# Second layer's tails in small pieces with ScalarE a block behind VectorE, and the third layer's scaled nodes made in those tails

## The chip, the cores and the metric

One core of one Trainium2 chip runs the whole kernel. The metric is the device time of one execution in microseconds (us). Every time of a whole kernel below is the median of several executions in the fast state (no run of this study was slow); every profile is one fast execution. The engines are named as the profile names them: PE is TensorE's matmuls, PEld its weight loads, DVE is VectorE, ACT is ScalarE, POOL is GpSimd, SP is SyncE, which in these kernels only issues transfers. `SPq` and `ACTq` are the instruction queues in which SyncE and ScalarE issue DMA.

## The reference

Four graph layers over 4096 nodes of 128 features and a dense 4096 x 4096 adjacency of zeros and ones, each followed by a residual and a layer norm. The change touches the second layer (attention with four heads) and the start of the third (a normalised graph convolution).

```python
def _L1(x, adj, Wq, bq, Wk, bk, Wv, bv, Ws, bs, Wb):          # second layer
    q, k, v = (x @ W + b, split into 4 heads of 32)
    attn = einsum('nhc,mhc->hnm', q, k) / sqrt(32)
    e = where(adj == 0, 0, exp(attn - rowmax))
    out = (e / e.sum(-1)) @ v
    x_r = x @ Ws + bs                                          # the skip term
    beta = sigmoid(concat([out, x_r, out - x_r]) @ Wb)
    return beta * x_r + (1 - beta) * out

def _L2(x, adj, weight):                                       # third layer
    deg = sum(adj + I, axis=1)
    d = (deg + 1e-8) ** -0.5
    return relu((d[:, None] * (adj + I) * d[None, :]) @ x @ weight)

x = layernorm(x + _L1(x, ...))
x = layernorm(x + _L2(x, ...))
```

## The kernel before

The second layer's attention runs over eight row blocks `I` of 512 nodes, each in 32 steps `jb` of 128 columns. The loop issues the scores two steps ahead of the sums (their lead), and hands one piece of the last row block's tail (a Python generator, one piece up to each `yield`) to every step. In the trace the engines take their instructions in the order in which this loop emits them: in the first tail ScalarE exponentiated scores that were there at 1144.18 us only from 1146.29, after a wait of 3.35 us at `be`, and TensorE began sums whose mask had ended at 1164.54 only at 1166.71, after scores that had waited 2.24 us for ScalarE. The last row block has no steps after it: its tail runs alone, and is called drained below. The passage from the last sums to the end of the third layer's first row is called the handover.

```python
def degree():                       # one half row block of adjacency, summed by ScalarE
    nc.scalar.activation(nat, nat, AF.Identity, accum_out=self.deg2[:, k, i : i + 1])
    row(n + 1)                      # the next load, into the same (single) buffer

def scores(I, jb):
    e = ep.tile([P, NH, S], F32, tag="e", name="e")
    for h2 in range(0, NH, 2):
        p = ps_s.tile([P, 2, S], F32, tag="s", name="ps")        # three buffers
        ...  # two matmuls
        nc.scalar.activation(e[:, h2 : h2 + 2, :], p, AF.Exp)
    nc.vector.scalar_tensor_tensor(e, at..., 0.0, e, op0=ALU.not_equal, op1=ALU.mult)   # the mask

def ending(I):                      # the tail of a row block
    ev = ...                        # ScalarE copies the sums out
    r = R[:, 4 * I : 4 * I + 4, :]  # the skip terms of this row block
    yield
    for a in range(2):
        ...  # 4 transposes, maximum, reciprocal, 4 products into o
        yield
    for b in range(4):
        ...  # two products with the gate's weights, summed into be
        yield
    nc.vector.tensor_tensor(be[:, 0, :], be[:, 0, :], be[:, 1, :], ALU.add)
    nc.scalar.activation(be[:, 0, :], be[:, 0, :], AF.Exp, scale=-1.0)       # waits for the line above
    yield
    ...  # the gate: 1 + be, reciprocal, 1 - be
    for b in range(4):
        ...  # X += r * beta + o * (1 - beta), then the row's mean and variance
        yield
    nc.vector.tensor_scalar(rs, self.mv[:, 4 * I : 4 * I + 4, 1], EPS_LN, None, op0=ALU.add)
    nc.scalar.activation(rs, rs, AF.Ln)                                      # waits for the line above
    nc.scalar.activation(rs, rs, AF.Exp, scale=-0.5)
    yield
    for b in range(4):
        ...  # X = (X - mean) * rs

for n in range(-LEAD, len(seq)):    # LEAD = 2
    I, jb = seq[n + LEAD]
    if jb % 4 == 3 and (I or jb > 8) or I == NS - 1 and jb in (13, 17):
        degree()
    scores(I, jb)
    I, jb = seq[n]
    sums(I, jb)
    next(rest, None)                # one piece of the tail
    if jb == NT - 1:
        rest = ending(I); next(rest)

def layer2(self, weight):           # the third layer
    nc.vector.tensor_scalar(d, d, 1.0, 1e-8, op0=ALU.add, op1=ALU.add)
    nc.scalar.activation(d, d, AF.Sqrt)
    nc.vector.reciprocal(d, d)
    for t in range(NT):             # 32 instructions
        nc.vector.tensor_scalar(Y[:, t, :], X[:, t, :], d[:, t : t + 1], None, op0=ALU.mult)
    for I in range(NS):
        ...  # 4 matmuls with the identity
        for J in range(NS):
            (nc.sync if J % 2 else nc.scalar).dma_start(out=at, in_=self.adjT[I, J])
            ...  # 4 matmuls pa += Y^T at
```

Of the kernel before, what the change touches and what calls it, by code (L numbers as in the profile page):

```python
# [16 lines left out]
P = 128  # L17
# [13 lines left out]
class Net:  # L31
# [737 lines left out]
    def layer1(self, Wq, bq, Wk, bk, Wv, bv, Ws, bs, Wb):  # L769
# [4 lines left out]
        with ExitStack() as ctx:  # L774
# [11 lines left out]
            R = keep.tile([P, NT, D], F32, tag="R", name="R")  # L786
# [81 lines left out]
    def attention_unshifted(self, VA, KS, QS, at0, stack, R, wb):  # L868
# [4 lines left out]
        with ExitStack() as ctx:  # L873
# [72 lines left out]
            def ending(I):  # L946
# [10 lines left out]
                for a in range(2):  # L957
# [6 lines left out]
                    nc.vector.reciprocal(sm[:, a, :, :], sm[:, a, :, :])  # L964
                    for b in range(4):
                        nc.vector.tensor_tensor(
                            o[:, b, :].rearrange("p (c h) -> p h c", h=NH)[:, 2 * a : 2 * a + 2, :],
                            pt[:, b, :].rearrange("p (g c) -> p g c", g=2)[:, :, 0:C],
                            sm[:, a, :, b].unsqueeze(2).to_broadcast([P, 2, C]),
                            ALU.mult,  # L970
                        )
                    yield
                for b in range(4):
                    for k, t in enumerate((o, r)):
                        junk = rot.tile([P, D], F32, tag="junk", name="junk")
                        nc.vector.scalar_tensor_tensor(
                            junk, t[:, b, :], 1.0, wb[k], op0=ALU.mult, op1=ALU.mult, accum_out=be[:, k, b : b + 1]
                        )
                    yield

                nc.vector.tensor_tensor(be[:, 0, :], be[:, 0, :], be[:, 1, :], ALU.add)
                nc.scalar.activation(be[:, 0, :], be[:, 0, :], AF.Exp, scale=-1.0)
# [3 lines left out]
                nc.vector.tensor_scalar(be[:, 1, :], be[:, 0, :], -1.0, 1.0, op0=ALU.mult, op1=ALU.add)  # L986
                for b in range(4):
                    x = X[:, 4 * I + b, :]
                    nc.vector.scalar_tensor_tensor(x, r[:, b, :], be[:, 0, b : b + 1], x, op0=ALU.mult, op1=ALU.add)
                    nc.vector.scalar_tensor_tensor(x, o[:, b, :], be[:, 1, b : b + 1], x, op0=ALU.mult, op1=ALU.add)  # L990
                    self.row_stats(4 * I + b)
                    yield
                nc.vector.tensor_scalar(rs, self.mv[:, 4 * I : 4 * I + 4, 1], EPS_LN, None, op0=ALU.add)
                nc.scalar.activation(rs, rs, AF.Ln)
                nc.scalar.activation(rs, rs, AF.Exp, scale=-0.5)
                yield
                for b in range(4):
# [3 lines left out]
                    )  # L1001

            seq = [(I, jb) for I in range(NS) for jb in range(NT)]
            LEAD = 2
            rest = iter(())
            with tc.manual_schedule():
# [33 lines left out]
            nc.vector.tensor_tensor(self.deg, self.deg2[:, 0, :], self.deg2[:, 1, :], ALU.add)  # L1040
# [106 lines left out]


    def layer2(self, weight):
        nc, tc, N, NT, NS, D, X = self.nc, self.tc, self.N, self.NT, self.NS, self.D, self.X  # L1150
        with ExitStack() as ctx:
            keep = ctx.enter_context(tc.tile_pool(name="keep2", bufs=1))
            rot = ctx.enter_context(tc.tile_pool(name="rot2", bufs=2))
            at2 = ctx.enter_context(tc.tile_pool(name="at2", bufs=8))
            ps_a = ctx.enter_context(tc.tile_pool(name="ps_a", bufs=2, space=PSUM))
            ps_b = ctx.enter_context(tc.tile_pool(name="ps_b", bufs=2, space=PSUM))
            Y = keep.tile([P, NT, D], F32, tag="Y", name="Y")
            w = self.load_mat(weight, "w2")

# [4 lines left out]
            for t in range(NT):  # L1164
                nc.vector.tensor_scalar(Y[:, t, :], X[:, t, :], d[:, t : t + 1], None, op0=ALU.mult)
            for I in range(NS):
# [11 lines left out]
                for J in range(NS):  # L1178
                    at = at2.tile([P, 4, S], F32, tag="at", name="at")
                    (nc.sync if J % 2 else nc.scalar).dma_start(out=at, in_=self.adjT[I, J])  # L1180
# [227 lines left out]
def tile_kernel(  # L1408
# [11 lines left out]
    net.layer1(Wq, bq, Wk, bk, Wv, bv, Ws, bs, Wb)  # L1420
    net.layer2(w2)
# [30 lines left out]
```

## Time and profile before

| what | value |
|---|---|
| time before the study | 2402.70 us, median of 3 runs (2401.38 to 2403.52) |
| profiled run | span 2398.1 us |
| busy share of the span | PE 84%, DVE 79%, ACT 61% |
| the second layer's attention | about 1022 to 1842 us of the span |
| a row block in it (copies `ev` to copies `ev`) | 102.5 to 102.9 us |
| last sums of the attention to the end of the third layer's first row | 57.9 us (1841.62 to 1899.51) |

The two rows of the page's costliest groups that matter most are TensorE's sums and scores in the second layer. The columns are line, engine, operation, tiles, shapes and count; then busy us and mean ns of one; then the idle time just before them with what ended it.

```profile
L937 PE MATMUL pv<-e,VA 128*64 128x512 f32 x2048 | 501.8, 611 | 8.0 <-DVE e L920 8.0
L911 PE MATMUL ps<-QS,KS 128*128 128x512 f32 x1024 | 315.1, 427 | 26.3 <-ACT e L918 24.2
```

Directly visible idle time of TensorE is only some 34 us. The change can be worth more than that: after 2.24 us of idle time in the first tail, eight sums took 2.84 us in place of 1.94, and that cost hides in the busy time. (Each of the code's four matmuls with sums is two records in the trace, hence eight; so it is with `pa`.) The lines that carry the argument from here are shown in the prediction; ScalarE's table load (`ACT_TABLE_LOAD`) at 1859.06, of which it speaks, took 1.28 us, and from 1130 to 1858 us, where the tails' Ln and Exp lie, there is none.

### The profile page before, as it was taken

The numbers are of one execution on the slowest core, as the hardware profiler recorded it, in microseconds if no ns is written. First come the engines' busy times: TensorE is split into PE (matmuls) and PEld (weight loads), VectorE is DVE, ScalarE is ACT, GpSimd is POOL, SyncE is SP. The second block draws the span as 40 slices with busy tenths as digits, with TensorE's granted clock in tenths as the row PEclk, the third lists the DMA queues.
The fourth block names the chain that finished last, engine by engine and source line by source line (L and its number), as shares of the span: only waits on it lengthen the run. The fifth ranks groups of instructions, "written<-read, shape, count | busy, mean of one in ns | idle before, by whom it ended". The sixth has DMA issues, their size and how long they took to land.

```text
span 2398.1 us, 24121 instructions
## 1 busy us (share of the span) xinstructions
PE 2018.2 (84%) x8795; PEld 1117.5 (47%) x8795; DVE 1901.2 (79%) x2695; ACT 1459.8 (61%) x1761; POOL 107.1 (4%) x146
## 2 busy tenths in 40 slices
PE   4477878778777761799999999999997899979998
PEld 4266666566666651533333333333332444444443
DVE  7478888788788888777787878778786877668887
ACT  5688899888888886478777787777875000010000
POOL 2000000000000042221000000000000000000000
PEclk7689989989898895799999999999999899989999
DMA  2455466564656530697464564645453877537884
GB/s 53 141 181 196 154 206 205 160 206 156 201 175 193 177 126 1 228 226 213 159 192 158 176 193 158 192 149 186 171 180 124 315 285 286 200 123 285 290 291 170
DMA packets 112869, 448.45 MB, mean 187 GB/s; under 512 B 9760, under 2 KB 20064, under 8 KB 71776
## 3 DMA queue, kind: packets, MB, share of 16 engines
q1 hardware_dynamic: 84944, 294.71, 36.3%
q10 hardware_dynamic: 18576, 135.27, 16.1%
q0 software_dynamic: 9216, 16.78, 3.9%
q8 instruction: 73, 1.20, 0.2%
q14 instruction: 60, 0.49, 0.1%
HBM read 369.10 MB, written 77.63 MB: 186 GB/s over the span
## 4 chain that ended last, share of the span: by engine, by line
PE 56%; DVE 25%; ACT 12%; issue 3%; DMA 2%; ACTq 0%; POOL 0%; SPq 0%; DVEq 0%; POOLq 0%
PE pv L937 15%; PE pa L1327 9%; PE pa L1182 9%; PE ps L911 9%; DVE e L920 5%; PE pz L583 4%; DVE w L606 3%; PE pi L674 3%; DVE w L636 3%; DVE t L632 3%; PE ptA L564 3%; ACT t L628 3%; ACT e L918 2%; ACT at L572 2%; ACT w L601 1%
## 5 line engine op out<-in xcount | busy, mean ns | idle before, releaser
L920 DVE SCALAR_TENSOR_TENSOR e<-at,e 128x2048 f32<-128x2048 f32 x256 | 581.6, 2287 | 169.0 <-ACT e L918 168.5
L918 ACT ACTIVATE e<-ps 128x1024 f32<-128x1024 f32 x512 | 489.2, 1025 | 132.0 <-PE ps L911 103.4
L937 PE MATMUL pv<-e,VA 128*64 128x512 f32 x2048 | 501.8, 611 | 8.0 <-DVE e L920 8.0
L911 PE MATMUL ps<-QS,KS 128*128 128x512 f32 x1024 | 315.1, 427 | 26.3 <-ACT e L918 24.2
L911 PEld LDWEIGHTS ps<-QS,KS 128*128 128x128 f32 x1024 | 172.2, 190 | 254.8 <-ACT e L918 167.1
L674 PE MATMUL pi<-HA,w 128*128 128x129 f32 x1152 | 188.1, 339 | 84.1 <-DVE w L636 84.1
L937 PEld LDWEIGHTS pv<-e,VA 128*64 128x64 f32 x2048 | 125.8, 137 | 252.6 <-issue 227.5
L1327 PE MATMUL pa<-w,F 128*128 128x512 f32 x512 | 223.8, 598 | 13.1 <-DVE w L1324 13.1
L1182 PE MATMUL pa<-at,Y 128*128 128x512 f32 x512 | 223.5, 597 | 4.1 <-DMA at<-adjT 4.1
L674 PEld LDWEIGHTS pi<-HA,w 128*128 128x128 f32 x1152 | 181.2, 251 | 94.4 <-DVE w L636 94.4
L1324 DVE SCALAR_TENSOR_TENSOR w<-rho,col,at 128x512 f32<-128x512 f32 x256 | 187.5, 747 | 19.3 <-PE pa L1327 2.3
L591 DVE SCALAR_TENSOR_TENSOR t<-ei,de,pz 128x512 f32<-128x512 f32 x144 | 107.4, 747 | 106.1 <-PE pz L583 102.3
L564 PE MATMUL ptA<-ident,ad 128*128 128x128 f32 x1032 | 145.8, 287 | 41.2 <-ACT at L572 34.1
L1192 DVE SCALAR_TENSOR_TENSOR odd<-at 128x2048 f32<-128x2048 f32 x64 | 146.5, 2290 | 37.8 <-DMA at<-adjT 37.2
L564 PEld LDWEIGHTS ptA<-ident,ad 128*128 128x128 f32 x1032 | 124.7, 148 | 97.5 <-ACT at L572 51.9
L572 ACT COPY at<-ptA 128x512 f32<-128x512 f32 x200 | 108.4, 588 | 98.7 <-PE ptA L564 98.5
L583 PE MATMUL pz<-HT 128*128 128x512 f32 x292 | 161.5, 664 | 4.9 <-DVE w L655 4.6
L1327 PEld LDWEIGHTS pa<-w,F 128*128 128x128 f32 x512 | 97.6, 192 | 135.0 <-issue 105.0
L1182 PEld LDWEIGHTS pa<-at,Y 128*128 128x128 f32 x512 | 97.6, 192 | 124.4 <-issue 119.5
L606 DVE TENSOR_TENSOR w<-w,at 128x2048 f32<-128x2048 f32 x64 | 143.7, 2281 | 0.0
L1331 ACT COPY a<-pa 128x512 f32<-128x512 f32 x8 | 4.7, 586 | 202.0 <-PE pa L1327 178.8
L903 ACT ACTIVATE nat<-nat 128x2048 f32<-128x2048 f32 x64 | 122.7, 1918 | 3.2 <-DMA nat<-in_adj_dram 3.2
(341 smaller groups left out, 2368.8 us busy)
## 6 DMA issues: line engine op xcount, KB each, us to landing
at<-adjT SPq DMA_DIRECT2D x127, 1024.0 KB, 4.8
at<-adjT ACTq DMA_DIRECT2D x65, 1024.0 KB, 4.9
ad<-in_adj_dram SPq DMA_DIRECT2D x64, 1024.0 KB, 6.4
adjT<-at SPq DMA_DIRECT2D x64, 1024.0 KB, 8.3
nat<-in_adj_dram ACTq DMA_DIRECT2D x64, 1024.0 KB, 4.9
qk<-cut SPq DMA_DIRECT2D x16, 512.0 KB, 11.7
KS<-qk POOLq DMA_DIRECT2D x32, 256.0 KB, 8.9
QS<-qk POOLq DMA_DIRECT2D x32, 256.0 KB, 8.5
```

The lines of the kernel that those rows point to most:

```text
L564: nc.tensor.transpose(pt[:, ib, :], st[p]["ad"][k][:, ib, jb * P : (jb + 1) * P], self.ident)
L572: copy(st[p]["at"][k][:, jb, :], st[p]["pt"].pop(m))
L583: nc.tensor.matmul(pz, lhsT=HT[:, j * P : (j + 1) * P], rhs=HT[:, I * S : (I + 1) * S], start=True, stop=True)
L606: nc.vector.tensor_tensor(w, w, at, ALU.mult)
L674: nc.tensor.matmul(self.po[ib // 2][:, ib % 2, :], lhsT=w[0][:, jb, ib * P : (ib + 1) * P], rhs=HA[:, 4 * J + jb, :], start=False, stop=(J ...
L911: nc.tensor.matmul(p[:, h, :], lhsT=KS[:, h2 + h, jb * P : (jb + 1) * P], rhs=QS[I % 2][:, h2 + h, :], start=True, stop=True,)
L918: nc.scalar.activation(e[:, h2 : h2 + 2, :], p, AF.Exp)
L920: nc.vector.scalar_tensor_tensor(e, at[:, jb % 4, :].unsqueeze(1).to_broadcast([P, NH, S]), 0.0, e, op0=ALU.not_equal, op1=ALU.mult,)
L937: nc.tensor.matmul(st["po"][h // 2][g : g + 64, :], lhsT=VA[:, o : o + 64], rhs=e[:, h, :], start=(jb == 0), stop=(jb == NT - 1), skip_gro ...
L1182: nc.tensor.matmul(pa, lhsT=Y[:, 4 * J + jb, :], rhs=at[:, jb, :], start=False, stop=(J == NS - 1 and jb == 3), skip_group_check=True,)
L1324: nc.vector.scalar_tensor_tensor(w, rho[:, I * S : (I + 1) * S], col[:, 0, j : j + 1], at[:, jb, :], op0=ALU.max, op1=ALU.mult)
L1327: nc.tensor.matmul(pa, lhsT=F[:, j, :], rhs=w, start=False, stop=(j == NT - 1), skip_group_check=True)
```

## The change

Its intent: no ScalarE instruction of a tail should have to wait for a VectorE instruction emitted in the same piece (ScalarE comes one step later, the lag of the runs below), no piece should be longer than what VectorE has free in a step, and the work in front of the third layer (degrees to the power -1/2, 32 scalings) should lie in the tails, where VectorE has room. The scaled nodes overwrite the skip terms `R`, which are dead by then, so they need no memory of their own. The description of the change counts 30 pieces; by the `yield`s there are 25, and 14 before, with the copies `ev` counted in both.

```diff
@@ the tail
                     nc.vector.reciprocal(sm[:, a, :, :], sm[:, a, :, :])
+                    yield
                     for b in range(4):
...
-                for b in range(4):
-                    for k, t in enumerate((o, r)):
+                for k, t in enumerate((o, r)):
+                    for b in range(4):
...
-                    yield
+                        if b % 2:
+                            yield
                 nc.vector.tensor_tensor(be[:, 0, :], be[:, 0, :], be[:, 1, :], ALU.add)
+                yield
                 nc.scalar.activation(be[:, 0, :], be[:, 0, :], AF.Exp, scale=-1.0)
                 yield
...  # yields also after the gate and between update and statistics of each row
-                nc.vector.tensor_scalar(rs, self.mv[:, 4 * I : 4 * I + 4, 1], EPS_LN, None, op0=ALU.add)
+                nc.vector.tensor_scalar(rs, self.mv[:, tl, 1], EPS_LN, None, op0=ALU.add)
+                nc.vector.tensor_tensor(d[:, tl], self.deg2[:, 0, tl], self.deg2[:, 1, tl], ALU.add)
+                nc.vector.tensor_scalar(d[:, tl], d[:, tl], 1.0, 1e-8, op0=ALU.add, op1=ALU.add)
+                yield
                 nc.scalar.activation(rs, rs, AF.Ln)
                 nc.scalar.activation(rs, rs, AF.Exp, scale=-0.5)
+                nc.scalar.activation(d[:, tl], d[:, tl], AF.Ln)
+                nc.scalar.activation(d[:, tl], d[:, tl], AF.Exp, scale=-0.5)
                 yield
...  # the normalisation in two pieces
+                for b in range(4):
+                    t = 4 * I + b
+                    if b % 2 == 0:
+                        yield
+                    nc.vector.tensor_scalar(R[:, t, :], X[:, t, :], d[:, t : t + 1], None, op0=ALU.mult)
@@ the third layer
-    def layer2(self, weight):
+    def layer2(self, weight, Y):                  # Y is R, now allocated outside the second layer
-            Y = keep.tile([P, NT, D], F32, tag="Y", name="Y")
-            nc.vector.tensor_scalar(d, d, 1.0, 1e-8, op0=ALU.add, op1=ALU.add)
-            nc.scalar.activation(d, d, AF.Sqrt)
-            nc.vector.reciprocal(d, d)
-            for t in range(NT):
-                nc.vector.tensor_scalar(Y[:, t, :], X[:, t, :], d[:, t : t + 1], None, op0=ALU.mult)
...
-                    (nc.sync if J % 2 else nc.scalar).dma_start(out=at, in_=self.adjT[I, J])
+                    (nc.scalar if J % 2 else nc.sync).dma_start(out=at, in_=self.adjT[I, J])
```

More of the change, by code (lines that the diff above doesn't have):

```diff
@@ L766, in pair_loop, with layer1 @@
                     step(p)
-    def layer1(self, Wq, bq, Wk, bk, Wv, bv, Ws, bs, Wb):
+    def layer1(self, Wq, bq, Wk, bk, Wv, bv, Ws, bs, Wb, R):
         nc, tc, N, NT, D, X = self.nc, self.tc, self.N, self.NT, self.D, self.X
@@ L785, in layer1 @@
             qk = self.dram.tile([2, 2, P, N], F32, tag="qk", name="qk")
-            R = keep.tile([P, NT, D], F32, tag="R", name="R")
             wb = [self.load_row(Wb[k * D : (k + 1) * D, 0], f"wb{k}") for k in range(3)]
@@ L972, in ending @@
                     yield
-                for b in range(4):
-                    for k, t in enumerate((o, r)):
+                tl = slice(4 * I, 4 * I + 4)
+                for k, t in enumerate((o, r)):
+                    for b in range(4):
                         junk = rot.tile([P, D], F32, tag="junk", name="junk")
@@ L990, in ending @@
                     nc.vector.scalar_tensor_tensor(x, o[:, b, :], be[:, 1, b : b + 1], x, op0=ALU.mult, op1=ALU.add)
+                    yield
                     self.row_stats(4 * I + b)
-                    yield
-                nc.vector.tensor_scalar(rs, self.mv[:, 4 * I : 4 * I + 4, 1], EPS_LN, None, op0=ALU.add)
+                    if b < 3:
+                        yield
+                nc.vector.tensor_scalar(rs, self.mv[:, tl, 1], EPS_LN, None, op0=ALU.add)
+                nc.vector.tensor_tensor(d[:, tl], self.deg2[:, 0, tl], self.deg2[:, 1, tl], ALU.add)
+                nc.vector.tensor_scalar(d[:, tl], d[:, tl], 1.0, 1e-8, op0=ALU.add, op1=ALU.add)
+                yield
                 nc.scalar.activation(rs, rs, AF.Ln)
                 nc.scalar.activation(rs, rs, AF.Exp, scale=-0.5)
+                nc.scalar.activation(d[:, tl], d[:, tl], AF.Ln)
+                nc.scalar.activation(d[:, tl], d[:, tl], AF.Exp, scale=-0.5)
                 yield
@@ L1001, in ending @@
                     )
+                    if b == 1:
+                        yield
+                for b in range(4):
+                    t = 4 * I + b
+                    if b % 2 == 0:
+                        yield
+                    nc.vector.tensor_scalar(R[:, t, :], X[:, t, :], d[:, t : t + 1], None, op0=ALU.mult)
             seq = [(I, jb) for I in range(NS) for jb in range(NT)]
@@ L1005, in attention_unshifted @@
             rest = iter(())
+            d = self.deg
             with tc.manual_schedule():
@@ L1039, in attention_unshifted @@
                     pass
-            nc.vector.tensor_tensor(self.deg, self.deg2[:, 0, :], self.deg2[:, 1, :], ALU.add)
     def attention_shifted(self, V, qk, R, wb, spare):
@@ L1146, in attention_shifted @@
             self.normalise()
-    def layer2(self, weight):
-        nc, tc, N, NT, NS, D, X = self.nc, self.tc, self.N, self.NT, self.NS, self.D, self.X
-        with ExitStack() as ctx:
-            keep = ctx.enter_context(tc.tile_pool(name="keep2", bufs=1))
-            rot = ctx.enter_context(tc.tile_pool(name="rot2", bufs=2))
-            at2 = ctx.enter_context(tc.tile_pool(name="at2", bufs=8))
-            ps_a = ctx.enter_context(tc.tile_pool(name="ps_a", bufs=2, space=PSUM))
-            ps_b = ctx.enter_context(tc.tile_pool(name="ps_b", bufs=2, space=PSUM))
-            Y = keep.tile([P, NT, D], F32, tag="Y", name="Y")
-            w = self.load_mat(weight, "w2")
             d = self.deg
@@ L1164, in layer2 @@
             for t in range(NT):
-                nc.vector.tensor_scalar(Y[:, t, :], X[:, t, :], d[:, t : t + 1], None, op0=ALU.mult)
+                nc.vector.tensor_scalar(R[:, t, :], X[:, t, :], d[:, t : t + 1], None, op0=ALU.mult)
+    def layer2(self, weight, Y):
+        nc, tc, N, NT, NS, D, X = self.nc, self.tc, self.N, self.NT, self.NS, self.D, self.X
+        with ExitStack() as ctx:
+            at2 = ctx.enter_context(tc.tile_pool(name="at2", bufs=8))
+            rot = ctx.enter_context(tc.tile_pool(name="rot2", bufs=2))
+            ps_a = ctx.enter_context(tc.tile_pool(name="ps_a", bufs=2, space=PSUM))
+            ps_b = ctx.enter_context(tc.tile_pool(name="ps_b", bufs=2, space=PSUM))
+            w = self.load_mat(weight, "w2")
+            d = self.deg
             for I in range(NS):
@@ L1419, in tile_kernel @@
     net.layer0(x, w0, b0, attw, attb)
-    net.layer1(Wq, bq, Wk, bk, Wv, bv, Ws, bs, Wb)
-    net.layer2(w2)
+    with tc.tile_pool(name="scaled", bufs=1) as pool:
+        Y = pool.tile([P, net.NT, net.D], F32, tag="Y", name="Y")
+        net.layer1(Wq, bq, Wk, bk, Wv, bv, Ws, bs, Wb, Y)
+        net.layer2(w2, Y)
     net.layer3(w3, b3, a_s, a_r, out)
```

## The prediction

> **What bounds the kernel now**
>
> I read the page's busy shares first. TensorE is busy 84% of the span and the chain that ended last is 56% TensorE, but these are averages over four layers. So I asked which stretch holds the changed lines. The second layer's attention runs from 1022 to about 1842 us in eight row blocks of 32 steps; each step makes scores (L911), exponentiates them on ScalarE (L918), masks them on VectorE (L920) and sums them (L937), with scores two steps ahead of sums. A finished row block's tail is carried by the steps of the next. The busy times by stretch (columns: stretch, then busy us and count on PE, weight loads, DVE, ACT, POOL; clock; DMA share; GB/s) show one row block's tail, then its quiet rest:
>
> ```profile
> 1174.00:1225.00 51.00, 51.00 (x206) 19.70 (x204) 39.16 (x18) 41.17 (x45) 2.14 (x4) 1.00 0.60 184
> 1225.00:1277.00 52.00, 48.18 (x190) 18.35 (x188) 42.98 (x69) 36.63 (x42) 0.00 (x0) 0.97 0.48 164
> ```
>
> In the quiet part TensorE has no gap: it is the bound, at 2.994 us a step (scores begin at 1173.23 and, 18 steps on, the pass ends at 1227.16 in the chain: 53.93 / 18). In the tail it idles 3.8 of 52 us and its clock dips to 0.97, though DVE (43) and ACT (37) have room. So the tail loses time by waits, not work. The timeline of the first tail shows which:
>
> ```profile
> 1145.99 0.15 DVE L981 TENSOR_TENSOR be<-be 128x4 f32<-128x4 f32 x1
> 1146.18 0.21 ACT L982 ACTIVATE be<-be 128x4 f32<-128x4 f32 x1 [3.35 <-DVE be L981]
> ...
> 1157.82 1.94 PE L937 MATMUL pv<-e,VA 128*64 128x512 f32 x8 [0.30 <-DVE e L920]
> ...
> 1164.45 0.16 DVE L993 TENSOR_SCALAR rs<-mv 128x4 f32<-128x4 f32 x1
> 1164.65 0.20 ACT L994 ACTIVATE rs<-rs 128x4 f32<-128x4 f32 x1 [5.62 <-DVE rs L993]
> ...
> 1166.05 0.72 PE L911 MATMUL ps<-QS,KS 128*128 128x512 f32 x2 [2.24 <-ACT e L918]
> 1166.71 2.84 PE L937 MATMUL pv<-e,VA 128*64 128x512 f32 x8
> ```
>
> The four-element ScalarE instruction stands behind a DVE instruction that itself stands behind a 2.29 us mask. ScalarE stands still for 3.35 and 5.62 us, no exponential is made, and TensorE starves 2.24 us, then runs slowly (2.84 us for eight matmuls that take 1.94). Lost against 2.994 us a step, from the starts of the scores: 0.92 at `be`, 1.24 over the X steps (3.37 to 3.45 us each: mask 2.2 plus four small instructions 1.17), 3.40 at `rs`, 0.69 in the slow step after: 6.25 us.
>
> The copies `ev` mark the same point of each row block: 1120.85, 1223.69, 1326.60, 1429.51, 1532.37, 1635.02, 1737.51, so periods of 102.84, 102.91, 102.91, 102.86, 102.65 and 102.49. Ideal is 32 x 2.994 = 95.81, plus 0.39 for each of two transpose groups that stay (1124.65 to 1128.03 is 3.38): 96.6. Excess: 6.2 on average, in all six. In the last row block, scores from 1737.90 to 1833.87 hold 8.4 us of excess: its degree sums come every second step, and each waits for its own single-buffered load.
>
> Last I read the handover to the third layer, in the chain in order of time and the timeline:
>
> ```profile
> 1853.04 0.04 ACT rs L995
> 1853.08 5.98 issue
> 1859.06 0.75 ACT L1162
> ...
> 1860.23 9.17 DMA at<-adjT
> 1869.40 0.04 issue
> 1869.45 30.92 PE pa L1182 x66
> ```
>
> ```profile
> SPq L1180 <- DVE X L989: 34.6, 1, 34.6
> ```
>
> The conditional ends, ScalarE needs 5.98 us to come to its next instruction, loads a table, issues adjacency block 0, and TensorE has that at 1869.45. SyncE, idle, waited 34.6 us for L989, the last reader of the skip terms R, before it issued blocks 1, 3, 5, 7 at 1851.76; these then shared the transfer rate with block 0, which took 9.17 instead of the usual 4.8 us.
>
> [...] DVE 83% and ACT 70% busy in the tail, bubbles on PE. [...] the trace has 1.28 us at 1859.06 and no load at the present Ln, so the new Ln and Exp cost no switch. [...] The trace has 5.98 us on ACT and 5.16 on DVE after the conditional; [...] the change leaves it.
>
> **The change part by part**
>
> *Smaller pieces.* I count 25 pieces by the yields (13 before, last two joined), so a tail still fits in 32 steps. The DVE budget of a step is 2.994 - 2.29 = 0.70 us. Pieces, by cadence in the trace: two X instructions 0.73 (1154.31 to 1155.06), statistics 0.45, two beta products 0.54, four `o` products 0.54, maximum and reciprocal 0.43, two normalisations 0.56, two scalings of the third layer 0.4 to 0.56. All but one fit, with the mask overlapping (2.17 + 0.73 = 2.9). The exception is last statistics, rs, and two degree instructions: 0.45 + 3 x 0.2 = 1.05, 0.35 over, while the next piece holds nothing for DVE. So the 1.24 goes.
>
> *ACT a block behind.* `be`: its sum is made a step earlier, and a degree sum (2.47 us) lies before the scores between, so ScalarE comes late enough: 0.92 goes. `rs`: now four instructions, 4 x 0.24 = 0.95. Here the step behind a degree sum is the bad one: worked from the quiet sequence at 1821 to 1837, exponentials run back to back after the degree sum, the two masks follow late, and rs with its two degree companions is ready about 1.3 us after ScalarE asks. ScalarE is about 1.4 late afterwards, of which the next degree step can hide some 0.6 to 0.8 (DVE's lead there over the sums, 1828.2 to 1829.01). I leave 0.8 of loss in each tail. Hence 6.2 - 0.8 = 5.4 in each of six row blocks: 32.
>
> *Last row block.* Its degree sums at steps 11, 13, 15, 17, 19 come 7.2 us apart (1766.57 to 1773.74) where two steps are 6.0: 4 x 1.2 = 4.7 stays lost, less about 1.5 of lead. 8.4 - 3.2 - 0.8 = 4.4. Together 36.8 us.
>
> *Scaling moved.* Y's 32 instructions (6.36 us at 1861.21), the Sqrt and its table load leave the path in front of layer three; 28 of the scalings and all but the last degree work lie in DVE slack. The last tail, drained with nothing beside it, gains 2 DVE degree instructions (0.4), 2 on ACT (0.48) and 4 scalings, so ScalarE ends about 0.9 later: 1854.2.
>
> *R in an outer pool, queues swapped.* SyncE no longer waits for R, only for what lies under the new buffers (V and the keys, last read by the sums that end at 1841.6), and has block 0. Estimate: blocks 0, 2, 4, 6 issued near 1843, 10 us at the 415 GB/s that the handover's slices reach, all there by 1854. TensorE does block 0 inside the tail. ScalarE issues block 1 at 1854.2 + 5.8 + 0.4 = 1860.4, alone on the rate: there at 1865.2. Seven blocks from there: 7 x 3.43 + 3.4 [...] = 1892.7, where the row ended at 1900.4: gain 7.7 on that clock; some doubt of the early issue, 7.
>
> Sum: 36.8 + 7 = 43.8, less some for what I did not see: 43. 2402.7 - 43 = 2359.7, so 2360.
>
> **The rivals**
>
> 1. *Waits move instead of going.* PSUM: the transposed sums now keep one of three score buffers over a yield, so two remain for about two steps more, next to the `ev` copies and a degree sum. For it: the weight loads of the scores already wait mostly for ACT (167 us over the run). Against: the same two-buffer steps in the present tail (1124 to 1137) run at 2.99. If it held and rs waited longer, 2 to 2.5 us a tail stay: total about 2369.
> 2. *Everything hides.* Loss per tail zero and the start as above: 37 + 5.5 + 8 = 50.5, so 2352. For it: DVE and ACT have 9 and 15 us of room in the tail; against: in-order ScalarE with degree sums every fourth step.
> 3. *The loads stay late.* If SyncE still waits until about 1852, block 1 shares the rate again: the handover brings 5 instead of 7, 2362. If TensorE also had to wait for the last scaled node, about 4.
> 4. *DVE becomes the bound of the tail*: 12 us of tail work plus 2 us new in 25 steps x 0.70 = 17.5 of room; an X step at 3.0 or 3.1 would cost 1 us a tail, 2366. Not slower than before.
>
> **Range and chances**
>
> The ceiling of about 51 us makes 2% (48 us, 2354.6) reachable only if nearly nothing is left; the likely residues give 33 to 47. Range 2351 to 2371. Faster by over 2%: 0.22; within: 0.76; slower: 0.02 (a false dependency by the shared tile, nothing in the code suggests one).
>
> **What would show it right or wrong**
>
> `ev` copies 97.0 to 98.0 us apart in the first six periods confirm the tails; 99 or more refutes. The `be` wait of ScalarE should be near 0, that of `rs` 1 to 1.5 in place of 5.62. X steps at 2.99. On the changed kernel's own clock the tails come out about 37 us earlier, so what counts at the handover is distance: SyncE's first adjacency load issued within 2 us of the last sums (10 us behind them now), TensorE on block 0 before ScalarE's first load, that load landing in about 4.8 us, and the first row of the third layer ending some 51 us after the last sums (1900.4 - 1841.6 = 58.8 now). I would be wrong in the large if third-layer matmuls of later rows, or the fourth layer, changed: I expect 29.36 us a row there, as now.

## The result, and the profile after

| | before | after |
|---|---|---|
| median | 2402.04 us (2399.61 to 2403.52, 4 runs) | 2357.77 us (2356.13 to 2360.83, 4 runs) |
| ratio | 1 | 0.9818 (95%: 0.9801 to 0.9835) |
| span of the profiled run | 2398.1 | 2354.3 |

A ratio here is the mean time of one kernel's fast runs over that of the other kernel's fast runs of the same rounds, so it is not quite the ratio of the medians quoted beside it. 1.8% faster falls within the 2% that the prediction called most likely, and 2357.8 is 2 us under the predicted 2360.

Two stretches of the changed kernel, one row block's tail and then its quiet part, with the columns of the two shown of the kernel before (those stand the other way round, the quiet part first, although the sentence above them names the tail first):

```profile
1122.00:1174.00 52.00, 52.00 (x213) 20.52 (x214) 44.39 (x59) 41.37 (x46) 0.00 (x0) 1.00 0.57 188
1174.00:1225.00 51.00, 50.88 (x208) 19.76 (x207) 42.25 (x37) 41.98 (x49) 2.14 (x4) 1.00 0.63 188
```

TensorE now has no gap in the tail either, 213 matmuls where a tail of before held 190, at full clock. The second stretch shows VectorE at 42.25 where before it had 39.16: the later pieces of the tail reach into it.

The timeline of one tail, the lines that answer to those of `be` and `rs` before:

```profile
1249.53 0.15 DVE L985 TENSOR_TENSOR be<-be 128x4 f32<-128x4 f32 x1
...
1250.89 0.20 ACT L987 ACTIVATE be<-be 128x4 f32<-128x4 f32 x1
...
1280.82 0.20 ACT L1005 ACTIVATE rs<-rs 128x4 f32<-128x4 f32 x1 [1.15 <-DVE rs L1001]
...
1281.08 1.94 PE L938 MATMUL pv<-e,VA 128*64 128x512 f32 x8
```

ScalarE comes to the gate 1.2 us after VectorE has made its sum, so the 3.35 us wait is gone; at `rs` 1.15 us of wait are left of 5.62, and the sums after it run at 1.94 us, not 2.84. The copies `ev` now stand 97.21 to 97.23 us apart.

The chain of waits at the handover, which showed `issue` 5.98, then 9.17 for the load, before:

```profile
1817.98 2.83 issue
...
1821.28 5.64 DMA at<-adjT
...
1827.06 25.79 PE pa L1200 x56
```

And in the timeline there, the first issue on SyncE's queue and what TensorE did (ScalarE's first load is the one at 1821.28 above):

```profile
1807.52 17.59 SPq L1198 DMA_DIRECT2D at<-adjT  x5
...
1813.36 5.15 PE L1200 MATMUL pa<-at,Y 128*128 128x512 f32 x8
...
1827.06 3.47 PE L1200 MATMUL pa<-at,Y 128*128 128x512 f32 x4 [8.55 <-DMA at<-adjT]
```

SyncE issues its first block 1.3 us after the last sums (1806.18), and TensorE multiplies block 0 inside the drained last tail. Then it stands still for 8.55 us, because the next block is on ScalarE's queue, and ScalarE is still in the tail and then in the 2.83 us after the conditional.

Where the 43.8 us between the two profiled runs lie, from the starts and ends of the same groups in both traces:

| stretch | before | after | difference |
|---|---|---|---|
| start to first copy `ev` | 1120.85 | 1121.46 | +0.61 |
| first to seventh `ev` (six row blocks) | 616.66 | 583.31 | -33.35 |
| seventh `ev` to the end of the last sums | 104.11 | 101.41 | -2.70 |
| last sums to end of the third layer's first row | 57.89 | 46.66 | -11.23 |
| the third layer's other rows | | | +0.86 |
| preparation of the fourth layer | 47.77 | 50.05 | +2.28 |
| fourth layer | | | -0.26 |
| sum | | | -43.79 |

The fourth layer's preparation runs the same matmuls in the same order, some of them slower: eight matmuls `psr` take 5.29 us in place of 3.68, seventeen transposes 3.54 in place of 2.33. In the runs below the eight take 3.68 or between 5.08 and 5.75, and both values occur among kernels with the change (3.68 where ScalarE's Ln comes later or where the lag is taken out, 5.31 where the degree sums are spread). The granted clock goes with it: 0.69 over the eight (2079.4 to 2084.8 us), where before it was 1.00 (2124.0 to 2127.7). What sets it apart is open.

### The profile page after: what moved, and what is told of

The parts are those of the page before. It is cut to its first block, busy times and chain, and to the rows that moved or that the text cites. A ratio compares the mean times of both kernels' runs of the same rounds, so it can differ in the third digit from the quotient of the medians.

```text
span 2354.3 us, 24080 instructions
## 1 busy us (share of the span) xinstructions
PE 2013.7 (86%) x8795; PEld 1118.5 (48%) x8795; DVE 1896.6 (81%) x2708; ACT 1463.7 (62%) x1777; POOL 106.9 (5%) x146
## 4 chain that ended last, share of the span: by engine, by line
PE 60%; DVE 21%; ACT 13%; issue 3%; DMA 2%; ACTq 0%; SPq 0%; POOL 0%; DVEq 0%; POOLq 0%
PE pv L938 16%; PE ps L912 10%; PE pa L1345 9%; PE pa L1200 9%; PE pz L583 4%; DVE w L606 3%; PE pi L674 3%; DVE t L632 3%; DVE w L636 3%; PE ptA L564 3%; ACT t L628 3%; ACT at L572 2%; ACT e L919 2%; DVE e L921 2%; ACT w L601 1%
## 5 line engine op out<-in xcount | busy, mean ns | idle before, releaser
L642 PE MATMUL ptz<-ident,t 128*128 128x128 f32 x448 | 68.7, 294 | 67.7 <-DVE w L655 45.8
## 6 DMA issues: line engine op xcount, KB each, us to landing
qk<-cut SPq DMA_DIRECT2D x16, 512.0 KB, 11.8
```

## The experiments

Twelve runs were made, in three groups, each group on one chip with the kernel before beside it. All results were correct.

### Group one: which half of the change does what, and which half of the tail's part

**Tails only.** The kernel before with the changed tail (small pieces and lag), without the degrees and the scalings in it, and with the third layer as before.

```diff
 # kernel before, ending(): the changed kernel's yields and order
-nc.vector.tensor_tensor(d[:, tl], self.deg2[:, 0, tl], self.deg2[:, 1, tl], ALU.add)   # and the other
-...                                                                                     # degree lines
-    nc.vector.tensor_scalar(R[:, t, :], X[:, t, :], d[:, t : t + 1], None, op0=ALU.mult)
```

> The kernel before with the small pieces and ScalarE one block behind, and nothing else of the change: the skip terms stay skip terms, the scaling and the queues of the third layer stay as they were. Theory (the gain is mostly waits of ScalarE and oversize pieces in the tails): the changed kernel's trace gives 33.4 us between the first and the seventh copy ev and 2.7 us in the last row block, so about 36, a little more because rs has two ScalarE instructions less behind it; ev about 97.1 us apart; ratio to before 0.985, and the handover takes as long as before (about 58 us from the last sums to the end of the first row of matmuls). Rival (the moved scaling is what carries the gain, the pieces only make room for it): under 15 us, ratio above 0.994.

Measured: 2363.51 us (2360.21 to 2373.26, 5 runs), ratio 0.9855 (0.9832 to 0.9879). The first six row blocks took 96.88 to 97.16 us each, the last 101.0 to the end of the last sums (before: 104.1), the handover 56.2 (before: 57.9). So the tails carry four fifths of the gain.

**Handover only.** The changed kernel with the coarse tails of before, without lag; the degrees join the `rs` piece, the scalings follow as one more piece.

```diff
 # changed kernel, ending(): the yields of before, then
+                yield
+                for b in range(4):
+                    nc.vector.tensor_scalar(R[:, t, :], X[:, t, :], d[:, t : t + 1], None, op0=ALU.mult)
```

> The changed kernel with the old coarse tail pieces and no extra block between VectorE and ScalarE, but with the scaled nodes made in the tails, R in the outer pool and the swapped queues. Theory: the handover gains the 11 us that the changed kernel's trace shows, and each of seven tails loses about 0.5 us more than before, because two more ScalarE instructions (0.45 us) stand in the rs wait: net about 7 to 8, ratio 0.9967, ev 103.3 to 103.5 us apart. Rival (the handover's gain is only the early start of block 0, or needs the new pieces): under 4 us net, ratio above 0.998.

Measured: 2395.15 us (2392.76 to 2402.62, 22 runs), ratio 0.9971 (0.9963 to 0.9979). Row blocks 102.83 to 103.23, a mean of 103.02 against 102.78 before, so the tails lost about half of what I had expected; handover 47.4 us. The two halves together, 1.45% + 0.29% = 1.74%, make 1.81% within their intervals: they hardly touch each other.

**Lag only.** The kernel before with nothing but two `yield`s.

```diff
                 nc.vector.tensor_tensor(be[:, 0, :], be[:, 0, :], be[:, 1, :], ALU.add)
+                yield
                 nc.scalar.activation(be[:, 0, :], be[:, 0, :], AF.Exp, scale=-1.0)
...
                 nc.vector.tensor_scalar(rs, self.mv[:, 4 * I : 4 * I + 4, 1], EPS_LN, None, op0=ALU.add)
+                yield
                 nc.scalar.activation(rs, rs, AF.Ln)
```

> The kernel before with two more yields only, one ahead of the Exp of be and one ahead of the Ln of rs, so that ScalarE comes one block behind VectorE; the pieces stay coarse. Theory (by my sum of the losses of a tail: be 0.92, rs 3.40 and 0.69, X steps 1.24): the be and rs losses go but for half a microsecond, the X steps stay at 3.37 us: 4.4 of 6.2 us a tail, with a smaller share in the last row block about 29 us in all, ratio 0.988, ev 98.5 us apart. Rival (VectorE's coarse pieces set the tail, the wait of ScalarE is only where it shows): under 12 us, ratio above 0.995.

Measured: 2364.26 us (2362.81 to 2367.38, 4 runs), ratio 0.9850 (0.9829 to 0.9870); row blocks of 97.04 us, every one of the first six. I had expected 98.5, because I believed the coarse pieces themselves to be too long for VectorE. They are (the masks of the update steps, in which X gets its rows, start 3.4 us apart), but TensorE loses almost nothing by it: two added lines do as much as the whole new tail.

ScalarE's two groups between 1122 and 1770 us show what is left of the waits, about 0.5 us a tail each:

```profile
L983 ACT ACTIVATE be<-be 128x4 f32<-128x4 f32 x7 | 1.4, 206 | 3.7 <-DVE be L981 3.7
...
L996 ACT ACTIVATE rs<-rs 128x4 f32<-128x4 f32 x7 | 1.4, 206 | 3.6 <-DVE rs L994 3.6
```

**No lag.** The changed kernel without those two `yield`s; its small pieces stay.

```diff
                 nc.vector.tensor_tensor(be[:, 0, :], be[:, 0, :], be[:, 1, :], ALU.add)
-                yield
                 nc.scalar.activation(be[:, 0, :], be[:, 0, :], AF.Exp, scale=-1.0)
...
                 nc.vector.tensor_scalar(d[:, tl], d[:, tl], 1.0, 1e-8, op0=ALU.add, op1=ALU.add)
-                yield
                 nc.scalar.activation(rs, rs, AF.Ln)
```

> The changed kernel without the two yields ahead of ScalarE's Exp of be and Ln of rs, all small pieces kept. Theory: both waits come back, about 2.3 us at be and 4 at rs, and TensorE loses about 3.5 us a tail: 24 us slower than the changed kernel, so ratio to before about 0.992, ev about 100.7 us apart. Rival (small pieces are enough, VectorE reaches the sums early so ScalarE waits little): under 5 us slower, ratio about 0.983.

Measured: 2407.12 us (2400.31 to 2416.96, 22 runs), ratio 1.0025 (1.0015 to 1.0036), row blocks of 101.96 to 105.28 us. A miss: with the small pieces and no lag the kernel is slower than it was, the gain of the handover included, although ScalarE's two waits (3.01 and 2.98 us) are shorter than before (3.35 and 5.62). The timeline shows what the shorter wait at `be` runs into:

```profile
1258.11 0.20 ACT L986 ACTIVATE be<-be 128x4 f32<-128x4 f32 x1 [3.01 <-DVE be L985]
1258.23 1.89 ACT L904 ACTIVATE nat<-nat 128x2048 f32<-128x2048 f32 x1
...
1261.70 0.73 PE L912 MATMUL ps<-QS,KS 128*128 128x512 f32 x2 [2.58 <-ACT e L919]
1262.36 3.31 PE L938 MATMUL pv<-e,VA 128*64 128x512 f32 x8
```

The next thing on ScalarE after the wait is not an exponential but a degree sum (`nat`), which with its read and its load takes another 2.5 us; the exponentials start at 1260.62. TensorE, with three buffers for scores, stands still for 2.58 us, and then its eight sums take 3.31 us in place of 1.94. The granted clock goes with it (the number after the five engines' busy times and counts is PEclk):

```profile
1262.00:1266.00 4.00, 4.00 (x11) 1.08 (x10) 3.07 (x5) 2.40 (x3) 0.00 (x0) 0.60 0.66 246
```

The clock was granted at 0.60 in the 4 us after the gap. But not every such gap has this sequel. One tail later, after the same wait and the same gap, the sums keep their 1.94 us:

```profile
1366.93 0.73 PE L912 MATMUL ps<-QS,KS 128*128 128x512 f32 x2 [2.58 <-ACT e L919]
...
1367.60 1.94 PE L938 MATMUL pv<-e,VA 128*64 128x512 f32 x8
```

Counted over the tails of all fourteen profiles, 38 gaps of TensorE lasted 1.81 to 2.58 us; 25 of them were followed by eight sums of 2.79 to 3.68 us, 13 by sums of 1.94. After all 51 gaps of 0.54 to 1.68 us the sums took 1.94 (smaller ones were not counted). What decides for a gap of the first kind is not shown.

To see what each kernel loses where, I worked out from the timelines the time from the start of one step's scores to the next, in one tail, that which follows the second copy `ev`; given is the excess over 2.994 us (group three's kernels are included):

| kernel | transposes | step with `be` and the next | update steps | step with `rs` and the next |
|---|---|---|---|---|
| before | 0.8 | 0.92 | 1.24 | 4.16 |
| lag only | 0.8 | 0 | 0.45 | 0 |
| tails only | 1.05 | 0 | 0 | 0.05 |
| changed | 1.05 | 0 | 0 | 0.39 |
| no lag | 1.05 | 4.49 | 0 | 3.93 |
| no lag, shifted (group three) | 1.05 | 1.17 | 0 | 3.80 |

The last tails aside, the tails of one kernel agree with this one within 0.3 us, except where a gap of over 1.8 us occurs: `be` without lag costs 2.85 us in two tails and 4.46 to 4.54 in four, `rs` there 2.28 to 3.93, with the shift 2.23 to 3.79, in the kernel before 3.75 to 4.15.

Three things are to be read here. The update steps lose 1.24 us in the kernel before, where, as I read it, the wait at `be` has just used up the two steps of lead; with the wait gone, the same coarse pieces lose 0.45. The small pieces remove that 0.45 and cost 0.25 where a tail starts (transposes and products now in separate pieces). And a wait of 3 us costs 0.92 in one kernel and 4.49 in another, of which some 1.6 go with the slow sums.

The degree sum behind the wait is not all of it. At `rs` in the run without lag four exponentials stand behind a wait of 2.98 us and the three small instructions after it, and that costs 3.93:

```profile
1290.82 0.20 ACT L1003 ACTIVATE rs<-rs 128x4 f32<-128x4 f32 x1 [2.98 <-DVE rs L1000]
...
1291.50 3.75 ACT L919 ACTIVATE e<-ps 128x1024 f32<-128x1024 f32 x4
...
1292.56 0.73 PE L912 MATMUL ps<-QS,KS 128*128 128x512 f32 x2 [2.02 <-ACT e L919]
1293.22 3.45 PE L938 MATMUL pv<-e,VA 128*64 128x512 f32 x8
```

### Group two: what the changed kernel still loses

**The changed kernel again**, as the measure for this group.

```diff
 # no edit
```

> The changed kernel itself, on the same chip as the next three, as their base: ratio to before 0.980 to 0.983, ev 97.2 us apart, 46 to 48 us from the last sums to the end of the first row of matmuls of the third layer.

Measured: 2360.45 us (2355.53 to 2362.42, 5 runs), ratio 0.9819 (0.9797 to 0.9840). Row blocks 97.24 to 97.27, last one 101.73 to the end of the last sums, handover 47.6.

**ScalarE's Ln one block later still.**

```diff
                 yield
+                yield
                 nc.scalar.activation(rs, rs, AF.Ln)
```

> The changed kernel with one more block between rs on VectorE and its Ln on ScalarE. Theory (the 1.15 us that ScalarE still waits at rs costs TensorE 0.39 us a tail, by the chain of the changed kernel): the wait goes to 0, ev come 96.8 to 96.9 us apart in place of 97.21, 2.7 us less in all, about a tenth of a per cent. Rival (the wait is hidden behind TensorE anyway and 97.21 has another cause): ev stay at 97.2.

Measured: 2357.64 us (2348.58 to 2361.69, 5 runs), ratio 0.9807 (0.9781 to 0.9832), row blocks of 97.15 us: 0.1 us each, where I had expected 0.3 to 0.4. The wait has gone, but the loss has not:

```profile
1286.54 0.21 ACT L1009 ACTIVATE deg<-deg 128x4 f32<-128x4 f32 x1
1286.66 1.90 ACT L904 ACTIVATE nat<-nat 128x2048 f32<-128x2048 f32 x1
...
1289.36 1.51 PE L912 MATMUL ps<-QS,KS 128*128 128x512 f32 x4
```

Now the four small instructions stand directly before a degree sum. The exponentials come late again, and the next scores take 1.51 us where 1.20 is usual; that step takes 3.31 us in place of the changed kernel's 3.38. Half a miss: taking the wait away does not bring back the last 0.3 us; by these lines ScalarE's work at that place keeps it.

**The last row block's degree sums spread.** Its ten degree sums at every third step up to step 29, in place of eight at every fourth and two extra between them.

```diff
-if jb % 4 == 3 and (I or jb > 8) or I == NS - 1 and jb in (13, 17):
+if jb % 4 == 3 and (I or jb > 8) and I < NS - 1 or I == NS - 1 and jb % 3 == 2 and jb < 30:
```

> The changed kernel with the ten degree sums of the last row block at every third step (2, 5, ... 29) in place of 3, 7, 11, 13, 15, 17, 19, 23, 27, 31. Theory (a load and its sum take 7.2 us, two steps are 6.0 and three 9.0): the last row block, 101.4 us from its ev to the last sums, comes to 97 or 98, so 3.5 to 4.5 us less, ratio to before about 0.980. Rival (ScalarE's total work bounds that row block, 10 sums of 2.47 us with 64 exponentials): under 1 us less.

Measured: 2354.87 us (2348.47 to 2355.97, 5 runs), ratio 0.9795 (0.9774 to 0.9817); the last row block took 97.76 us where it took 101.73 (in five profiles with the attention of the changed kernel or with the later Ln it took 100.8 to 101.7, so the gain is 3.1 to 4.0; the totals' intervals overlap). In the changed kernel that block still shows this, ScalarE waiting for the load of its next half row and TensorE for ScalarE:

```profile
1747.58 1.91 ACT L904 ACTIVATE nat<-nat 128x2048 f32<-128x2048 f32 x1 [1.82 <-DMA nat<-in_adj_dram]
...
1751.12 0.83 PE L912 MATMUL ps<-QS,KS 128*128 128x512 f32 x2 [1.80 <-ACT e L919]
1751.89 3.48 PE L938 MATMUL pv<-e,VA 128*64 128x512 f32 x8
```

A gap of 1.80 us here, and again the sums after it take 3.48 us. In the changed kernel's second profile the gap at this place is 1.61 us and the sums keep 1.94. In the spread kernel all sums of the last row block take 1.94. The loads, not the tail's pieces, held the last row block.

**The third layer's first row on SyncE alone.**

```diff
-(nc.scalar if J % 2 else nc.sync).dma_start(out=at, in_=self.adjT[I, J])
+(nc.scalar if J % 2 and I else nc.sync).dma_start(out=at, in_=self.adjT[I, J])
```

> The changed kernel with all eight adjacency blocks of the third layer's first row on SyncE, which is free when ScalarE still works at the last tail. Theory (ScalarE's first load, 15 us after the last sums, is what TensorE waits for: 8.55 us idle): blocks follow each other every 2.5 us from the last sums, TensorE goes on from block 0, the first row of matmuls ends about 37 us after the last sums in place of 46.7: 9 us less, ratio to before 0.978. Rival (TensorE would wait for the last scaled nodes, made at the very end of the last tail, or the blocks are not free yet): under 3 us less.

Measured: 2346.90 us (2345.53 to 2349.50, 5 runs), ratio 0.9769 (0.9750 to 0.9789); last sums to end of the row 36.7 us, where the changed kernel took 47.6. The whole row now runs inside the drained tail and the gap of ScalarE, without a stop:

```profile
1810.53 34.33 SPq L1198 DMA_DIRECT2D at<-adjT  x12
...
1816.37 29.55 PE L1200 MATMUL pa<-at,Y 128*128 128x512 f32 x64
```

So the changed kernel left more at the handover than it took there: half of its first row was on the queue of an engine that was busy with the tail.

### Group three: the position of a wait, the queues, and the best of all

**No lag, shifted.** The run without lag with one `yield` more ahead of the gate's sum. ScalarE's Exp then stands where the changed kernel has it, with exponentials behind it; it still waits for a VectorE instruction of its own piece.

```diff
 # no-lag kernel
+                yield
                 nc.vector.tensor_tensor(be[:, 0, :], be[:, 0, :], be[:, 1, :], ALU.add)
                 nc.scalar.activation(be[:, 0, :], be[:, 0, :], AF.Exp, scale=-1.0)
```

> The small pieces without lag, as in the slow run of this study, but with one more step ahead of the sum of the gate's logits, so that ScalarE's Exp stands where the changed kernel has it, no longer directly ahead of a degree sum; VectorE's sum is still in the same piece, so ScalarE still has to wait for it, by about as much (3 us). If it was the degree sum behind the wait that made the run without lag slow, a row block of the quiet part falls from 105.2 to 101 to 102.5, and the whole to 2382 to 2392 us (0.991 to 0.996). If the small pieces by themselves do the harm, it stays at 104.5 to 105.5 and 2403 to 2410.

Measured: 2385.38 us (2380.84 to 2388.94, 5 runs), ratio 0.9923 (0.9908 to 0.9937); row blocks 100.23 to 101.80 us, 101.24 on average, where the run without lag had 104.45. ScalarE waits more in sum than without the shift (2.43 + 4.00 a tail against 3.01 + 2.98), and the tail still loses 3.2 us less. At `be`:

```profile
1255.26 0.20 ACT L987 ACTIVATE be<-be 128x4 f32<-128x4 f32 x1 [2.43 <-DVE be L986]
1255.37 3.75 ACT L919 ACTIVATE e<-ps 128x1024 f32<-128x1024 f32 x4
...
1256.43 0.74 PE L912 MATMUL ps<-QS,KS 128*128 128x512 f32 x2 [0.89 <-ACT e L919]
1257.09 1.94 PE L938 MATMUL pv<-e,VA 128*64 128x512 f32 x8
```

TensorE's gap is 0.89 us in place of 2.58, and the sums after it keep their 1.94 us with the clock granted at 1.00 (1258 to 1262 us). Over the six tails the step at `be` falls from 3.9 us on average to 1.2, with the same small pieces: so at `be` the place of the wait made it dear, and not the small pieces. How much of that is the degree sum behind it, and how much the wait that became shorter by 0.58 us, these runs do not part. The shift also moves the update steps and `rs` by one step; `rs`, with exponentials behind it in both, still costs 3.3 us on average, against 3.6.

**The queues as before.** The changed kernel with even blocks of the third layer on ScalarE's queue again.

```diff
-(nc.scalar if J % 2 else nc.sync).dma_start(out=at, in_=self.adjT[I, J])
+(nc.sync if J % 2 else nc.scalar).dma_start(out=at, in_=self.adjT[I, J])
```

> The changed kernel with the queues of the third layer's blocks as before the change: even blocks on ScalarE's, odd ones on SyncE's. The theory: TensorE can no longer do block 0 inside the last tail and waits for ScalarE's first load before it does anything of the first row; only the time of one block, 3 to 4 us, comes on top, so the first row ends 50 to 51 us after the last sums (47.6 in the changed kernel's second measurement) and the whole is 2362 to 2365 us, about 0.983. Rival: the order of queues is worth nothing, as block 1 waits for ScalarE's load either way and TensorE catches up: the same as the changed kernel within 1 us.

Measured: 2361.61 us (2359.83 to 2365.45, 5 runs), ratio 0.9823 (0.9810 to 0.9837); last sums to end of row 50.4 us.

```profile
1830.96 3.75 PE L1200 MATMUL pa<-at,Y 128*128 128x512 f32 x4 [13.33 <-DMA at<-adjT]
```

TensorE does nothing of the first row before ScalarE's first load, and then all 64 matmuls. The swap is worth 2.8 us of the stretch (50.4 against 47.6; in two profiles of the changed kernel, and in those with the later Ln and the spread sums, it took 46.7 to 48.4). In the totals, against the kernel before, that small difference does not show above the intervals.

**All further edits together**: later Ln, spread degree sums, first row on SyncE.

```diff
 # changed kernel with the three edits of group two
```

> The changed kernel with three further edits together: ScalarE's Ln and Exp of a tail's variances one block later still, the last row block's ten degree sums spread over its blocks, and all eight first blocks of the third layer on SyncE's queue. Alone they gave 0.7, 4.0 and 10.9 us against the changed kernel's second measurement. If they are independent, as I hold, the last row block takes about 97.5 us, the stretch from the last sums to the end of the third layer's first row about 37, and the whole 2345 us (2342 to 2348), 0.976 of before. Rival: the handover's gain came partly out of the last row block's late degree sums (ScalarE's queue was then the late one), so that the two overlap: the whole then stays at 2347 to 2350.

Measured: 2340.64 us (2338.51 to 2346.38, 5 runs) beside 2404.87 before, ratio 0.9739 (0.9724 to 0.9753). The last row block took 96.8 us and the handover 35.7. The gains add up, and a little more: it lies below the 2342 to 2348 that I had expected, and beats both kernels. In its chain of waits at the handover TensorE runs the 64 records of the first row without a stop (1809.12 to 1837.72).

**The same with coarse tails**: the tail of before with the two `yield`s of the lag, the scaled nodes as one last piece, and the spread degree sums and SyncE for the first row.

```diff
 # handover-only kernel
+                yield        # ahead of ScalarE's Exp of the gate
+                yield        # ahead of ScalarE's Ln
 # and the spread degree sums, and the first row on SyncE
```

> The kernel of before's coarse tail with nothing but the two yields ahead of ScalarE's Exp and Ln, the scaled nodes as one separate last piece, the spread degree sums and SyncE for all of the first row. The theory (the lag does the work, the small pieces hardly any) says 97.0 to 97.4 us a row block in the quiet part and a total within 3 us of the run with the small pieces, 2345 to 2350. The rival (small pieces are needed once four more VectorE instructions lie in the tail) says 98.5 or more a row block and 2354 us or more.

Measured: 2343.44 us (2339.01 to 2343.76, 5 runs), ratio 0.9740 (0.9727 to 0.9754), row blocks of 97.02 to 97.04 us. It cannot be told from the version with small pieces. With the lag in place, cutting the tail finer buys nothing that these runs can show, even with the degrees and the scalings in it.

## Why the prediction was right or wrong

The total was right, 2360 against 2357.8, and the kind of answer too. That it came so close is partly luck: the terms below were off by +0.95, -1.7, +4.2 and -3.5 us, and nearly cancel.

**The tails: right in size, half wrong in their reason.** Predicted 5.4 us in each of six row blocks, 32.4; measured 33.35, or 5.56 each. The residue at `rs` was put at 0.8 and came out at 0.39; the predicted wait of 1 to 1.5 us there is 1.15, the `be` wait is gone, and the periods of 97.2 lie in the predicted 97.0 to 98.0. But the step "The exception is last statistics ... So the 1.24 goes", which gave the update steps' 1.24 us to the smaller pieces, failed: with lag alone the coarse pieces lose 0.45. Of the 1.24 us the lag removes 0.79; the pieces remove the 0.45, and give 0.25 back at the start of the tail. The argument compared a piece's length with what VectorE has free in one step, as if no lead stood between VectorE and TensorE. A two-step lead carried four steps of VectorE at about 3.4 us with 0.45 us lost, but, as the kernel before suggests, not once a wait had emptied it.

**The last row block: mechanism right, a term mis-sized.** Predicted gain 4.4, measured 2.70. The waits for the degree sums' loads were named; the term of it that failed is "4 x 1.2 = 4.7 stays lost, less about 1.5 of lead". By the starts of the scores, the steps with the loads lose 0.51, 3.71 and 0.53 us, 4.75 in sum, and the step at `rs` 0.70, where 3.2 and 0.8 were entered; 0.25 more goes at the start of the tail. So the lead of 1.5 us saved nothing: about all of the 4.7 was lost. How it falls on the steps differs by execution: here most lies in the one step with the gap of 1.80 us and the slow sums after it, in the changed kernel's second profile the steps lose 0.61, 1.88, 0.92 and 1.65 with no slow sums, 5.1 in sum. Spreading the sums brought back 3.1 to 4.0 us.

**The handover: mechanism right, mis-sized by 4.2 us.** Predicted 7.7, entered as 7; measured 11.23. SyncE's first load went out 1.3 us after the last sums and TensorE did block 0 inside the tail, as predicted. By terms, predicted against measured from the last sums on: ScalarE's end of the tail 12.6 against 11.8; its gap after the conditional 5.8 against 2.83; issue 0.4 against 0.47; landing 4.8 against 5.64; from there to the end of seven blocks 27.4 against 25.79 and 0.14 before it. (3.4 of the 27.4 stood for slow first matmuls: in the trace of before, the first weight loads after 1869.45 come 0.85 to 0.86 us apart and those from 1874.45 on 0.43, with the clock granted at 0.66 from 1869.4 to 1876.4 us and at 1.00 from 1876 to 1886. In the trace of the changed kernel it was 0.61 from 1827 to 1831 us and 1.00 from there to 1840.) The gap is the term that failed: it was carried over from the trace of before. In the eight profiles with the changed handover and half of the first row on ScalarE's queue the gap was 2.7 to 4.1 us, with coarse tails too (3.07), and 5.1 to 6.4 in the three with the handover of before. But in the three with the changed handover and the first row on SyncE alone, ScalarE's next instruction came 5.0 to 6.1 us after the conditional. So the scalings moved into the tails do not by themselves shorten the gap, and what does is open.

**What was not foreseen**: +0.61, +0.86, +2.28 and -0.26, in sum +3.5 us. Of the 0.86, 0.9 is a group of identity matmuls of the second row which before ran in TensorE's idle time. The 2.28 goes with TensorE's granted clock in the fourth layer's preparation (0.69 against 1.00 over the eight `psr`), and the cause of that is open.

So 32.4 + 4.4 + 7 = 43.8 was predicted, and 33.35 + 2.70 + 11.23 - 3.49 = 43.79 was measured.

**The rivals.** The first (waits move) is seen in a small form: the degrees' two more instructions at `rs` on each of VectorE and ScalarE cost 0.34 us a tail, 0.39 against 0.05 with tails only, far from 2 to 2.5. The second (everything hides, 2352) failed at the last row block and the unforeseen terms. The third (late loads) did not happen: the loads of SyncE were early. The fourth (VectorE as the bound) did not happen, and with the lag VectorE does not bind even in coarse pieces.

**Pieces, queue and gaps.** Small pieces paid in these runs only with an eye on the order in the queues (without lag 1.0025, the same pieces with one `yield` more 0.9923), and with the lag in place no more than coarse ones (0.9739 against 0.9740). What the whole case turns on is that an instruction that waits on ScalarE holds up the exponentials behind it (3.35 us at `be` and 5.62 at `rs` in the first tail of the kernel before). One thing was missing in the prediction: it saw the slow sums after one gap (2.84 us in place of 1.94), but not that gaps of the same length go both ways. Gaps of 1.81 to 2.58 us were followed by slow sums in 25 of 38 cases, gaps of 0.54 to 1.68 us in none of 51. What decides it is not shown.

## What to carry to other kernels

Before cutting work finer, look at what each small instruction waits for and at what stands behind it in its engine's queue: moving three small instructions of ScalarE by one step gave here what the whole rewritten tail gave (0.9850 against 0.9855), and waits of about 3 us (2.98 to 3.35) cost from 0.9 to 4.5 us, by their place in the queue and by the clock after them. Count a gap on TensorE not by its length alone but with the slow matmuls that can follow it: here they followed 25 of 38 gaps of 1.81 to 2.58 us and none of 51 of 0.54 to 1.68. Look at every tail for that, since the same gap went both ways within one trace. At a handover between stages, put the first transfers on the queue of an engine that has nothing else to finish: here the first row then ended 36.7 us after the last sums in place of 47.6.
